# A two-layer recurrent cell: the inverse square root taken as two GpSimd operations of two columns each, and another written-out order of the four streams' operations

## The chip, the cores and the metric

The kernel runs on one core of a Trainium2 chip. The metric is the device time of one execution in microseconds, given as the median of several executions. Work is spread over the core's engines: TensorE (PE, with its weight loads listed apart as PEld), VectorE (DVE), ScalarE (ACT), GpSimd (POOL), and SyncE (SP), whose queue issues most of the transfers. Each engine takes its own instructions strictly in the order in which the kernel lists them.

## What is computed

Four layers work on an array of 256 x 256 positions with 32 channels. The first three (a gated projection and two Sobel-like filters, each behind a group norm) are finished before the part that is changed. The last one is a recurrent network: the first axis counts 256 sequences, the second 256 time steps, and two cells of width H = 128 follow each other in every step. Cut to what matters:

```python
def step(carry, x_t):
    h_all, c_all = carry
    z = x_t @ W_lat + b_lat
    for j in range(2):                                   # two cells (layers)
        zz = concatenate([z, h_all[j]], axis=1) @ W_cell[j] + b_cell[j]
        zz = group_norm(zz)                              # 4 groups of 128: (zz - mu) * rsqrt(var + 1e-5)
        i, f, o, g = split(zz, 4, axis=1)
        c = sigmoid(f) * c_all[j] + sigmoid(i) * tanh(g)
        h = sigmoid(o) * tanh(c)
        z = z + h
    return (new_h, new_c), x_t + z @ W_out + b_out
```

The four groups of the norm are the four gates, so each gate of each sequence has one variance and one scale factor.

## The kernel before

**Streams.** The function `recurrence` (from line 1034) keeps four streams going: layer l (0 or 1) times half h (0 or 1) of the 256 sequences, so that 128 sequences fill the 128 partitions. Below, a name with two digits is an operation of one stream: `h01` is the operation `h` of layer 0, half 1. The means are folded into the weights, so the products in PSUM (`zz`, 128 x 512, four gates side by side) are already deviations from the group's mean.

**One step of a stream** is made by `one` (from line 1112). On PE: for layer 1 `i` (line 1130, the product with the lower layer's state), and `m` (line 1135, with the stream's own last state). Then `sq` (ACT, line 1143, squares of all four gates), `rd` (DVE, line 1148, four sums: tile `ve`, 128 x 4), and `pw` (POOL, line 1151: the power -0.5 of the four sums, tile `rs`, 128 x 4):

```python
rs = v["rs", l, h] = roots[:, 2 * l + h, t % slots, :]
nc.gpsimd.tensor_tensor(rs, get("ve"), inputs.mhalf, ALU.pow)
```

Column g of `rs` is then the scale of the gate activations `si`, `sf`, `so`, `tg` (ACT, line 1124; columns 0 to 3; the output gate's tile is `go`, the others share `ga`). DVE forms `ig` (line 1171), `fc` (line 1175) and the new cell state `c` (line 1179). Two forms end the step. Streams 00 and 10 turn first: PE transposes the output gate (`to`, line 1183) and the cell state (`T`, line 1187), ACT takes the tanh (`th`, line 1190), and DVE multiplies into the turned state hT (`h`, line 1193). Streams 01 and 11 take `th` from c, multiply (`h`, line 1197), transpose (`T`, line 1187), and DVE copies the result out (`e`, line 1199).

**Shared work.** `project` (lines 1100 and 1103; called PROJ below) starts the `zz` of all four streams once per step from the input. `both` (line 1210; `hs`) adds the two layers' states once per step. Once in eight steps `emit` makes the output: `o0` and `o1` (PE, lines 1222 and 1232), `of` (ACT, line 1241), `ot` (DVE, line 1247) and its transfers (line 1251).

**The order.** No scheduler orders this. The table PLAN gives each operation of each stream a due time, OUT those of the shared work; a step's times are shifted by PERIOD = 7.6 per step, all operations of the whole run are sorted by due time and issued in that order, so each engine's queue follows it. The due times are keys of a sort, not times of the chip. Taken modulo 7.6, the steady order in each queue is this (`o0`, `o1`, `of`, `ot` only in one step of eight):

- PE: PROJ m00 T11 i11 m11 to10 T01 i10 T10 m01 to00 (o0) m10 T00 (o1)
- ACT: so11 th11 (of) si01 tg01 sf01 so01 sq00 tg10 th01 so10 si10 sf10 sq11 sf00 so00 th10 si00 tg00 sq01 si11 sf11 tg11 th00 sq10
- DVE: rd10 (ot) h11 ig01 fc01 e11 c01 rd00 h01 ig10 fc10 e01 c10 rd11 fc00 h10 hs ig00 c00 rd01 fc11 ig11 h00 c11
- POOL: pw10 pw00 pw11 pw01

PSUM has eight banks, handed out first in, first out; `zz`, the transposes' target `pt` and the output's `px` each take one.

Of the kernel before, what the change touches and what calls it, by code (L numbers as in the profile page):

```python
# [14 lines left out]
ALU = mybir.AluOpType  # L15
# [4 lines left out]
T = 256  # L20
# [945 lines left out]
class RecurrentInputs:  # L966
# [34 lines left out]
    def of(self, t, rows):  # L1001
# [5 lines left out]


SLOTS = 32
PERIOD = 7.6  # L1010
BLOCKS = 2
PLAN = {
    (0, 0): dict(
        m=0.300, sq=1.315, rd=2.221, pw=2.435, sf=3.687, so=3.851, si=5.257, tg=5.350,
        fc=5.575, to=5.625, ig=5.913, c=6.078, T=7.351, th=7.469, h=7.525,
    ),
    (0, 1): dict(
        m=5.465, sq=5.522, rd=6.135, pw=6.225, si=8.272, tg=8.393, sf=8.539, so=8.617,
        ig=9.064, fc=9.178, c=9.275, th=9.750, h=10.406, T=11.076, e=11.164,
    ),  # L1020
    (1, 0): dict(
        i=11.801, m=14.599, sq=15.182, rd=15.403, pw=15.916, tg=17.278, so=17.665, si=17.826,
        sf=17.853, ig=18.025, to=18.521, fc=18.583, c=18.914, T=19.851, th=20.220, h=20.862,
    ),
    (1, 1): dict(
        i=17.726, m=17.895, sq=18.421, rd=19.343, pw=19.789, si=21.949, sf=21.973, fc=22.060,
        tg=22.379, ig=22.470, c=22.779, so=22.984, th=23.047, h=23.842, T=24.141, e=24.465,
    ),
}
OUT = dict(x=7.840, hs=28.575, o0=29.152, o1=30.235, of=30.667, ot=30.900)  # L1030

def recurrence(tc, out, ident, weights, inputs, general):

    nc = tc.nc
# [33 lines left out]
    def bank(name, key, shape):  # L1070

        k = held[key] = free.pop(0)
        return ps.tile(shape, F32, name=name, tag=f"bank{k}")

    def release(key):
        free.append(held.pop(key))
# [6 lines left out]
    def at(when, what, *args):  # L1083
        todo.append((when, len(todo), what, args))

    first = {k: min(ops[n] for n in ("i", "m") if n in ops) for k, ops in PLAN.items()}
    ahead = {k: floor((when - OUT["x"]) / PERIOD) for k, when in first.items()}
    streams = sorted(first, key=lambda k: first[k] - ahead[k] * PERIOD)

# [21 lines left out]
    def one(name, l, h, t):  # L1111
        seqs = slice(h * P, (h + 1) * P)
        turned = "to" in PLAN[l, h]
        get = lambda k: v[(k, l, h, t) if k == "zz" else (k, l, h)]
        gates = lambda x, g: x[:, g * H : (g + 1) * H]
        four = lambda x: x.rearrange("p (g m) -> p g m", g=4)

        def gate(g, func):

            x, scale = (get("zn"), 1.0) if general else (get("zz"), get("rs")[:, g : g + 1])  # L1120
            if g == 2:
                v["go", l, h] = up.tile([P, H], F32, name="go", bufs=8)
            dst = get("go") if g == 2 else gates(get("ga"), min(g, 2))
            nc.scalar.activation(dst, gates(x, g), func, scale=scale)  # L1124
            v["left", l, h, t] -= 1
            if not v["left", l, h, t]:
                release(("zz", l, h, t))

        if name == "i":
            nc.tensor.matmul(  # L1130
                get("zz"), lhsT=v["hT", 0, t][:, seqs], rhs=wc[:, l, 0, :], start=False, stop=t == 0
            )
        elif name == "m":
            if t:
                nc.tensor.matmul(  # L1135
                    get("zz"),
                    lhsT=v["hT", l, t - 1][:, seqs],
                    rhs=wc[:, l, 1, :],
                    start=False,
                    stop=True,  # L1140
                )
        elif name == "sq":
            nc.scalar.activation(  # L1143
                sqs[l, h, t % 2][:, :, 0:H], four(get("zz")), AF.Square, scale=float(H**-0.5)
            )
        elif name == "rd":
            ve = v["ve", l, h] = sums[:, 2 * l + h, t % slots, :]
            nc.vector.tensor_reduce(ve, sqs[l, h, t % 2], AX.X, ALU.add)  # L1148
        elif name == "pw":
            rs = v["rs", l, h] = roots[:, 2 * l + h, t % slots, :]  # L1150
            nc.gpsimd.tensor_tensor(rs, get("ve"), inputs.mhalf, ALU.pow)  # L1151
            v["ga", l, h] = up.tile([P, 3 * H], F32, name="ga")
            if not general:
                return
            zn = v["zn", l, h] = up.tile([P, 4 * H], F32, name="zn")
            for g in range(4):
                nc.vector.scalar_tensor_tensor(
                    gates(zn, g),
                    gates(get("zz"), g),
                    get("rs")[:, g : g + 1],  # L1160
                    gates(gam[:, l, :], g),
                    ALU.mult,
                    ALU.mult,
                )
            nc.vector.tensor_add(zn, zn, bet[:, l, :])
        elif name in ("si", "sf", "so", "tg"):
            g = ("si", "sf", "so", "tg").index(name)
            gate(g, AF.Tanh if name == "tg" else AF.Sigmoid)
        elif name == "ig":
            c = v["cn", l, h] = sp.tile([P, H], F32, name=f"c{l}{h}")  # L1170
            nc.vector.tensor_mul(c, gates(get("ga"), 0), gates(get("ga"), 2))  # L1171
        elif name == "fc":
            if t:
                fc = v["fc", l, h] = up.tile([P, H], F32, name="fc")
                nc.vector.tensor_mul(fc, gates(get("ga"), 1), get("c"))  # L1175
        elif name == "c":
            c = get("cn")
            if t:
                nc.vector.tensor_add(c, c, get("fc"))  # L1179
            v["c", l, h] = c  # L1180
        elif name == "to":
            v["pt", l, h] = bank("pt", ("pt", l, h), [P, 2, 2 * H])
            nc.tensor.transpose(get("pt")[:, 0, 0:P], get("go"), ident)  # L1183
        elif name == "T":
            if not turned:
                v["pt", l, h] = bank("pt", ("pt", l, h), [P, 2, 2 * H])
            nc.tensor.transpose(get("pt")[:, 1, 0:P], get("c" if turned else "h"), ident)  # L1187
        elif name == "th":
            th = v["th", l, h] = up.tile([P, H], F32, name="th", bufs=8)
            nc.scalar.activation(th, get("pt")[:, 1, 0:P] if turned else get("c"), AF.Tanh)  # L1190
        elif name == "h":
            if turned:
                nc.vector.tensor_mul(hidden(l, t)[:, seqs], get("pt")[:, 0, 0:P], get("th"))  # L1193
                release(("pt", l, h))
            else:
                hh = v["h", l, h] = up.tile([P, H], F32, name="h")
                nc.vector.tensor_mul(hh, get("go"), get("th"))
        elif name == "e":
            nc.vector.tensor_copy(hidden(l, t)[:, seqs], get("pt")[:, 1, 0:P])  # L1199
            release(("pt", l, h))  # L1200

    def hidden(l, t):
        if ("hT", l, t) not in v:
            v["hT", l, t] = hp.tile([P, S], F32, name=f"hT{l}", bufs=5 - l)
        return v["hT", l, t]
# [52 lines left out]
    for k in range(inputs.NX, NB // inputs.XT):  # L1258
        at(((k - inputs.NX + 1) * inputs.XT * J + 4.0) * PERIOD, inputs.load, k)
    at(-1e5, busy, 3)  # L1260
    for n in range(min(ahead.values()), T + max(ahead.values())):
        at(n * PERIOD + OUT["x"], project, n)
    for t in range(T):
        for (l, h), ops in PLAN.items():
            for name, when in ops.items():
                at(t * PERIOD + when, one, name, l, h, t)
        at(t * PERIOD + OUT["hs"], both, t)
    for blk in range(0, NB, BLOCKS):
        for part in ("o0", "o1", "of", "ot"):
            at(((blk + BLOCKS) * J - 1) * PERIOD + OUT[part], emit, blk, part)  # L1270
    todo.sort(key=lambda e: e[:2])
# [45 lines left out]
```

## Time and profile before

| what | value |
|---|---|
| median of 3 runs | 2505.21 us (2502.2 to 2510.31) |
| the profiled execution's own time | 2504.49 us |
| its span in the trace | 2502.6 us |
| mean granted TensorE clock | 0.992 of full speed |
| DVE busy | 2276.8 us (91%) |
| ACT busy | 2247.5 us (90%) |
| POOL busy | 1318.6 us (53%) |
| first `sq` of the recurrent part | at 551.10 us |
| starts of `pw00` from step to step | seven of 7.3 us, then one of 9.05 us, and so on |

In the rows of the timeline the columns are start, duration (both us), engine, line, operation, output <- inputs, shapes, count, and in brackets the idle time before it with what ended it. Neighbours on one engine may overlap: ACT, DVE and PE begin an instruction before the last has fully ended, so the time that an instruction takes from its engine is read from start to start. The groups of instructions give the busy time of a group and the mean ns of one. The chain of waits gives only start, duration, engine and line.

### The profile page before, as it was taken

Reading aid. Unit: us, or ns where it says so; the run is one execution under the profiler, and the core shown is the slowest. Engines: PE = TensorE matmul, PEld = TensorE weight load, DVE = VectorE, ACT = ScalarE, POOL = GpSimd, SP = SyncE. Lnnn points to the kernel's source line nnn. Section 1 sums busy time; section 2 is a strip of 40 time slices with the busy share of each in tenths; the row PEclk is TensorE's granted clock in tenths of the full one; section 3 lists DMA queues with packets and bytes.
Section 4 is the critical chain, followed back from the end, with each engine's and each line's share of the span. In section 5 each row is a group of like instructions: output and inputs, shape, how many; then the busy total and the mean of one; then the engine's idle time right before and its main releaser. Section 6 shows DMA issues by size and latency. Waiting matters only on the chain.

```text
span 2502.6 us, 41399 instructions
## 1 busy us (share of the span) xinstructions
PE 2462.8 (98%) x11615; PEld 1057.6 (42%) x11615; DVE 2276.8 (91%) x6644; ACT 2247.5 (90%) x6876; POOL 1318.6 (53%) x1347
## 2 busy tenths in 40 slices
PE   8999999989999999999999999999999999999997
PEld 4333466653444444444444444444444444444442
DVE  7798898969999999999999999999999999999997
ACT  6788676759999999999999999999999999999996
POOL 1344386845555555555555555555555555555553
PEclk9999999999999999999999999999999999999998
DMA  6877000020010101000010101010101010100000
GB/s 175 49 40 40 2 1 1 1 51 1 5 22 5 23 8 23 10 17 18 9 22 6 22 5 22 5 22 6 22 5 22 5 22 6 22 5 5 5 5 11
DMA packets 117556, 46.71 MB, mean 19 GB/s; under 512 B 77010, under 2 KB 110003, under 8 KB 117316
## 3 DMA queue, kind: packets, MB, share of 16 engines
q1 hardware_dynamic: 115940, 43.80, 12.5%
q8 instruction: 95, 1.56, 0.3%
q14 instruction: 145, 1.19, 0.2%
q10 hardware_dynamic: 1088, 0.13, 0.0%
q0 software_dynamic: 288, 0.03, 0.0%
HBM read 10.37 MB, written 8.39 MB: 7 GB/s over the span
## 4 chain that ended last, share of the span: by engine, by line
PE 77%; DVE 0%; ACT 0%; POOL 0%; issue 0%; DVEq 0%; POOLq 0%; ACTq 0%
PE zz L1135 37%; PE zz L1130 17%; PE zz L1103 9%; PE pt L1187 5%; PE zz L1100 3%; PE pt L1183 2%; PE px L1232 1%; PE px L1222 1%; POOL rs L1151 0%; DVE ve L1148 0%; ACT ga L1124 0%; ACT sq L1143 0%; PE px L1215 0%; DVE c L1171 0%; DVE fc L1175 0%
## 5 line engine op out<-in xcount | busy, mean ns | idle before, releaser
L1151 POOL TENSOR_TENSOR rs<-ve,mhalf 128x4 f32<-128x4 f32 x1024 | 1031.0, 1007 | 920.5 <-DVE ve L1148 920.5
L1135 PE MATMUL zz<-wc,hT 128*128 128x512 f32 x2040 | 1058.6, 606 | 0.7 <-DVE hT L1193 0.7
L1124 ACT ACTIVATE ga<-zz,rs 128x128 f32<-128x128 f32 x3072 | 972.6, 377 | 38.6 <-POOL rs L1151 9.6
L1148 DVE TENSOR_REDUCE ve<-sq 128x4 f32<-128x516 f32 x1024 | 703.5, 687 | 29.1 <-ACT sq L1143 8.0
L1143 ACT ACTIVATE sq<-zz 128x512 f32<-128x512 f32 x1024 | 628.9, 614 | 37.9 <-PE zz L1135 14.4
L1130 PE MATMUL zz<-wc,hT 128*128 128x512 f32 x1024 | 524.1, 594 | 0.0
L1135 PEld LDWEIGHTS zz<-wc,hT 128*128 128x128 f32 x2040 | 328.2, 189 | 398.1 <-DVE c L1179 167.6
L1124 ACT ACTIVATE go<-zz,rs 128x128 f32<-128x128 f32 x1024 | 393.9, 385 | 0.0
L1171 DVE TENSOR_TENSOR c<-ga 128x128 f32<-128x128 f32 x1024 | 299.0, 292 | 61.6 <-ACT ga L1124 31.7
L1179 DVE TENSOR_TENSOR c<-c,fc 128x128 f32<-128x128 f32 x1020 | 287.9, 282 | 9.0
L1175 DVE TENSOR_TENSOR fc<-ga,c 128x128 f32<-128x128 f32 x1020 | 291.9, 286 | 2.9 <-ACT ga L1124 2.9
L1103 PE MATMUL zz<-fx,xt 32*128 32x512 f32 x2048 | 265.6, 588 | 0.0
L472 DVE SCALAR_TENSOR_TENSOR o<-pa,wbias,sg 128x512 f32<-128x512 f32 x256 | 177.4, 744 | 29.7 <-ACT sg L468 19.8
L468 ACT ACTIVATE sg<-pa,wbias 128x512 f32<-128x512 f32 x256 | 160.1, 685 | 44.9 <-PE pa L459 40.2
L1187 PEld LDWEIGHTS pt<-ident,c 128*128 128x128 f32 x512 | 71.1, 139 | 285.1 <-DVE c L1179 276.8
L1190 ACT ACTIVATE th<-c 128x128 f32<-128x128 f32 x512 | 166.2, 325 | 0.4 <-DVE c L1179 0.4
L1190 ACT ACTIVATE th<-pt 128x128 f32<-128x128 f32 x512 | 145.9, 285 | 19.3 <-PE pt L1187 19.3
L1130 PEld LDWEIGHTS zz<-wc,hT 128*128 128x128 f32 x1024 | 161.0, 197 | 2.8 <-issue 0.5
L459 PE MATMUL pa<-xb,wg 32*128 32x512 f32 x512 | 157.7, 649 | 3.5 <-POOL xb L338 3.5
L1193 DVE TENSOR_TENSOR hT<-pt,th 128x128 f32<-128x128 f32 x512 | 145.9, 285 | 15.9 <-ACT th L1190 15.8
L1183 PEld LDWEIGHTS pt<-ident,go 128*128 128x128 f32 x512 | 71.5, 140 | 201.9 <-ACT go L1124 201.9
L1199 DVE COPY hT<-pt 128x128 f32<-128x128 f32 x512 | 145.1, 283 | 8.9 <-PE pt L1187 8.9
(193 smaller groups left out, 2894.4 us busy)
## 6 DMA issues: line engine op xcount, KB each, us to landing
xt<-xa SPq DMA_DIRECT2D x256, 64.0 KB, 2.0
rows<-rstd SPq DMA_DIRECT2D x128, 64.0 KB, 6.4
out_dram<-st SPq DMA_DIRECT2D x252, 32.0 KB, 1.7
nat<-in_x_dram SPq DMA_DIRECT2D x12, 512.0 KB, 10.4
half<-in_x_dram SPq DMA_DIRECT2D x8, 256.0 KB, 7.2
wc<-in_L_conv_W_cell_dram SPq DMA_DIRECT2D x2, 512.0 KB, 5.4
kt<-in_consts_dram SPq DMA_DIRECT2D x1, 640.0 KB, 3.9
kg<-in_consts_dram SPq DMA_DIRECT2D x1, 128.0 KB, 7.8
```

Of the source, the lines that this page charges most:

```text
L1103: nc.tensor.matmul(v["zz", l, h, t], lhsT=inputs.of(t, r), rhs=fx[r, :], start=False, stop=l == 0 and t == 0,)
L1124: nc.scalar.activation(dst, gates(x, g), func, scale=scale)
L1130: nc.tensor.matmul(get("zz"), lhsT=v["hT", 0, t][:, seqs], rhs=wc[:, l, 0, :], start=False, stop=t == 0)
L1135: nc.tensor.matmul(get("zz"), lhsT=v["hT", l, t - 1][:, seqs], rhs=wc[:, l, 1, :], start=False, stop=True,)
L1143: nc.scalar.activation(sqs[l, h, t % 2][:, :, 0:H], four(get("zz")), AF.Square, scale=float(H**-0.5))
L1148: nc.vector.tensor_reduce(ve, sqs[l, h, t % 2], AX.X, ALU.add)
L1151: nc.gpsimd.tensor_tensor(rs, get("ve"), inputs.mhalf, ALU.pow)
L1171: nc.vector.tensor_mul(c, gates(get("ga"), 0), gates(get("ga"), 2))
L1175: nc.vector.tensor_mul(fc, gates(get("ga"), 1), get("c"))
L1179: nc.vector.tensor_add(c, c, get("fc"))
L1187: nc.tensor.transpose(get("pt")[:, 1, 0:P], get("c" if turned else "h"), ident)
L1190: nc.scalar.activation(th, get("pt")[:, 1, 0:P] if turned else get("c"), AF.Tanh)
```

## The change

The power is taken in two operations: `pw` for columns 0 and 1 (gates si and sf), and a new operation `pwb` for columns 2 and 3 (so and tg). The table of due times is replaced throughout. Core of the diff (the branch `general` isn't taken with these inputs):

```diff
-PERIOD = 7.6
+PERIOD = 7.600
 PLAN = {
     (0, 0): dict(
-        m=0.300, sq=1.315, rd=2.221, pw=2.435, sf=3.687, so=3.851, si=5.257, tg=5.350,
-        fc=5.575, to=5.625, ig=5.913, c=6.078, T=7.351, th=7.469, h=7.525,
+        m=0.300, sq=1.475, rd=2.090, pw=2.888, pwb=3.419, si=3.769, sf=3.798, fc=4.338,
+        so=4.419, tg=4.493, ig=4.822, c=4.833, to=5.093, T=5.424, th=6.214, h=6.692,
     ),
     (0, 1): dict(
-        m=5.465, sq=5.522, rd=6.135, pw=6.225, si=8.272, tg=8.393, sf=8.539, so=8.617,
-        ig=9.064, fc=9.178, c=9.275, th=9.750, h=10.406, T=11.076, e=11.164,
+        m=4.605, sq=4.835, rd=5.086, pw=5.520, pwb=6.813, sf=7.880, si=7.991, tg=8.075,
+        so=8.101, fc=8.433, ig=8.752, c=9.517, th=9.888, h=10.336, T=10.648, e=11.260,
     ),
     (1, 0): dict(
-        i=11.801, m=14.599, sq=15.182, rd=15.403, pw=15.916, tg=17.278, so=17.665, si=17.826,
-        sf=17.853, ig=18.025, to=18.521, fc=18.583, c=18.914, T=19.851, th=20.220, h=20.862,
+        i=11.579, m=12.986, sq=13.883, rd=15.300, pw=15.346, sf=17.169, pwb=17.394, so=17.581,
+        si=17.706, tg=17.797, to=18.066, fc=18.100, ig=18.148, c=18.970, T=19.247, th=19.345,
+        h=19.660,
     ),
     (1, 1): dict(
-        i=17.726, m=17.895, sq=18.421, rd=19.343, pw=19.789, si=21.949, sf=21.973, fc=22.060,
-        tg=22.379, ig=22.470, c=22.779, so=22.984, th=23.047, h=23.842, T=24.141, e=24.465,
+        i=16.528, m=17.968, sq=18.616, rd=19.113, pw=19.749, pwb=19.886, si=20.050, sf=20.215,
+        fc=20.675, tg=20.941, ig=21.369, c=22.232, so=22.387, th=23.055, h=23.367, T=23.802,
+        e=24.421,
     ),
 }
-OUT = dict(x=7.840, hs=28.575, o0=29.152, o1=30.235, of=30.667, ot=30.900)
+OUT = dict(x=6.984, hs=31.315, o0=35.060, o1=35.991, of=38.590, ot=42.536)
...
         elif name == "pw":
             rs = v["rs", l, h] = roots[:, 2 * l + h, t % slots, :]
-            nc.gpsimd.tensor_tensor(rs, get("ve"), inputs.mhalf, ALU.pow)
+            now = slice(0, 4 if general else 2)
+            nc.gpsimd.tensor_tensor(
+                rs[:, now], get("ve")[:, now], inputs.mhalf[:, now], ALU.pow
+            )
...
+        elif name == "pwb":
+            if not general:
+                nc.gpsimd.tensor_tensor(
+                    get("rs")[:, 2:4], get("ve")[:, 2:4], inputs.mhalf[:, 2:4], ALU.pow
+                )
```

Sorted in the same way, the new due times give these queues:

- PE: m00 T11 i11 m11 to10 T01 i10 T10 m01 (o0) to00 m10 T00 (o1) PROJ
- ACT: th11 sf01 si01 tg01 so01 (of) sq00 sf10 th01 so10 si10 tg10 sq11 si00 sf00 th10 so00 tg00 sq01 si11 sf11 tg11 th00 sq10 so11
- DVE: rd10 h11 fc01 hs ig01 e11 c01 rd00 h01 fc10 ig10 e01 c10 rd11 fc00 h10 (ot) ig00 c00 rd01 fc11 ig11 h00 c11
- POOL: pw10 pwb10 pw00 pwb00 pw11 pwb11 pw01 pwb01

## The prediction

> **What bounds the kernel now.** I read the page first, for the share of each engine and the costliest groups; then the chain of waits in a stretch of the steady state, for what ends a step; then the timeline of the same stretch, to follow the one loss that I found there back to its source; last the rows of GpSimd alone, for the price of the new operation.
>
> The page, engines and the group of the changed operation:
>
> ```profile
> PE 2462.8 (98%) x11615; PEld 1057.6 (42%) x11615; DVE 2276.8 (91%) x6644; ACT 2247.5 (90%) x6876; POOL 1318.6 (53%) x1347
> ...
> L1151 POOL TENSOR_TENSOR rs<-ve,mhalf 128x4 f32<-128x4 f32 x1024 | 1031.0, 1007 | 920.5 <-DVE ve L1148 920.5
> ```
>
> PE is close to full. The power takes 1007 ns, 1024 times (4 streams x 256 steps), and POOL waits 920 us for its input: it is a link in a chain, not a bound.
>
> The chain of waits, two stretches (start, us, engine, line), one in a normal step, one in the step after an output:
>
> ```profile
> 1527.03 1.06 PE zz L1135 x2
> 1528.09 0.11 PE pt L1187
> 1528.20 0.86 PE zz L1130 x2
> 1529.06 0.86 PE zz L1135 x2
> 1529.92 0.11 PE pt L1183
> 1530.03 0.21 PE pt L1187
> ...
> 1536.19 1.05 PE zz L1135 x2
> ...
> 1539.08 0.11 PE pt L1183
> 1539.19 0.11 PE pt L1187
> ```
>
> The chain is PE throughout. A product takes 0.86, a transpose 0.11. Two rows are longer. m00 (1.06) stands right behind PROJ and loses 0.20; it loses the same (1.05) behind an output, where h00, its input, had ended 1.5 us before (1534.64 against 1536.12), so no order on the other engines cures that. T01 takes 0.21 in a normal step and 0.11 after an output: this 0.10 is a wait. It comes in seven steps of eight, which is why a normal step takes 7.30 and one with output 9.05 = 7.19 + 1.86 (o0 0.86, o1 1.00). So 0.10 x 7 x 32 = 22 us, some 25 with rounding, is all that any order or faster power can gain here while PE's work stays the same.
>
> The timeline, along T01's chain:
>
> ```profile
> 1511.61 1.01 POOL L1151 TENSOR_TENSOR rs<-ve,mhalf 128x4 f32<-128x4 f32 x1 [1.00 <-DVE ve L1148]
> 1512.38 0.31 ACT L1190 ACTIVATE th<-c 128x128 f32<-128x128 f32 x1
> 1512.64 0.88 ACT L1124 ACTIVATE ga<-zz,rs 128x128 f32<-128x128 f32 x3
> 1513.41 0.38 ACT L1124 ACTIVATE go<-zz,rs 128x128 f32<-128x128 f32 x1
> 1513.66 0.61 ACT L1143 ACTIVATE sq<-zz 128x512 f32<-128x512 f32 x1
> 1514.30 0.69 DVE L1148 TENSOR_REDUCE ve<-sq 128x4 f32<-128x516 f32 x1
> 1514.91 0.28 DVE L1197 TENSOR_TENSOR h<-go,th 128x128 f32<-128x128 f32 x1
> 1515.31 0.14 PEld L1187 LDWEIGHTS pt<-ident,h 128*128 128x128 f32 x1
> ```
>
> Read upward: T01's weights (h01) load at 1515.31; h01 stands behind rd00 on DVE (1514.30, and 0.61 from start to start); rd00 waits for sq00 (ends 1514.27); sq00 stands behind the four gates of stream 01 on ACT; the first gate starts at 1512.64, when pw01 ends (1512.62). Without the power it could start at 1512.58, for th11 starts at 1512.38 and a th of this kind holds ACT 0.20 (th01 1514.38, next 1514.58). The power's share in the loss is thus only 0.06; behind it waits ACT itself.
>
> **The price of half a power.** No row shows two columns. The bounds: 0.50 if all of it goes by the column, 1.01 if all is per instruction. Nearest rows, of the same 128x4 shape on POOL:
>
> ```profile
> 30.36 0.19 POOL L225 TENSOR_TENSOR mean_of<-ident,kg 128x4 f32<-128x4 f32 x1
> 30.49 0.30 POOL L226 MEMSET avg<- 128x256 f32 x1
> 30.86 1.03 POOL L228 COPY avg<-mean_of 128x4 f32<-128x4 f32 x8
> ```
>
> The same instruction with a cheap operation takes 0.19, and the next one starts 0.13 later. So 1.01 - 0.19 = 0.82 is the power proper. If it goes by column, a half spans 0.19 + 0.41 = 0.60, and the second starts 0.13 + 0.41 = 0.54 to 0.60 after the first. Against this stands a rule of the Trainium skill (GPSIMD Engine Reference, 3.1 Elementwise, side-by-side cycle accounting): about 2.6 cycles per element for two inputs, beside a fixed dispatch; at its 1.2 GHz an estimated 9 ns for four columns. By it nearly all of 1007 ns would be fixed, halves would cost 1.0 each, and POOL would need 8 x 1.0 = 8.0 us per step of 7.3. The rule is for an add, and the row of 0.19 shows that the fixed part of this shape is small; what it can't show is whether the power's 0.82 has a start-up of its own. I take 0.60, being nearest to the row.
>
> **The change, part by part.** PE's queue is the same round as before (PROJ only counts to the step before; o0 moves one place), so PE's work stays 7.19 per normal step plus the waits. The rest, in the times of the stretch above:
>
> - *Two halves.* Columns 0 and 1 are there at 1511.61 + 0.60 = 1512.21, columns 2 and 3 at about 1512.80. sf01 now starts when ACT is free, 1512.58; si01 follows at 1512.83, tg01 (first reader of the second half) at 1513.08, later than 1512.80; so01 1513.33; sq00 1513.58, above its other floor (m00 ends 1513.48). Then rd00 at 1513.58 + 0.61 + 0.03 = 1514.22, h01 0.61 later, 1514.83 in place of 1514.91. T01's wait falls by 0.07 to 0.08; I take 0.07, leaving 0.03.
> - *hs between fc01 and ig01.* hs holds DVE 0.34 (1509.86 to the next start 1510.20). fc01 (needs sf01, ended 1512.96) stands behind h11 at 1513.08, hs 1513.28, ig01 1513.62, e11 1513.82, c01 1514.02, and DVE is free at 1514.22: just when rd00 can start. I cost it at nothing, but the cover is used up, and each 0.01 more is 0.01 on T01. Bounds: no gain (rd00 can't start sooner), a loss of 0.07 if hs holds DVE for its full 0.41.
> - *Waits that are late next.* With T01 0.07 earlier, T10 needs c10: fc10, ig10, e01, c10 end at about 1516.12, weight load 1516.18, where 1516.26 suffices. to00 needs so00, now behind th10: 1516.72 + 0.36, load 1517.14, where 1517.22 suffices. m11 needs e11, 0.05 later than before, with some 0.12 to spare. Zero each, but none has more than 0.12.
> - *POOL.* 8 x 0.60 = 4.8 us in 7.3; in queue order pwb01 ends 1512.80, before rd10 gives pw10 its input at 1512.95. Nobody waits behind a half.
> - *of behind so01.* It holds ACT 0.57, once in eight steps, in a stretch where o0 and o1 keep PE back: before, sq00 stood idle 0.41 for m00 there although `of` had already been done. Zero; without that cover 0.6 x 32 = 18 us.
> - *ot between h10 and ig00.* This one isn't covered. ot holds DVE 0.64 (1535.87 to 1536.51). Before, it ran right behind an output's o1, with PE still late; now it runs nearly a step later, when the lead is used up. h10 at about 1516.86, ot 1517.07 to 1517.71, ig00 1517.71 (else 1517.37), c00 ends 1518.31, T00's load 1518.37 where 1518.19 suffices: +0.18, once in eight steps. Bounds 0 (if the lead of the output step lasts) and 0.34.
> - *Fill and drain* have the power in the open a few times; under 2 us, taken as zero.
>
> Sum per eight steps: -7 x 0.07 + 0.18 = -0.31; x 32 = -10 us. The profiled execution took 2504.5 (span 2502.6 and 1.9 around it), so 2494.6; the median lies 0.7 higher: 2495. With bounds of these terms (wait wholly gone, ot free: -0.70 x 32 = -22; wait halved, ot 0.34: -0.0): 2482 to 2505.
>
> **Rivals.**
> 1. *The power is mostly per instruction* (slower). Place: tg01, third gate of stream 01, waits for pwb01. With a half of x us it starts at 1511.61 + 2x, and from x = 0.73 on this is later than 1513.08; each 0.05 more costs 0.10 per step, and from about 0.77 the whole gain of T01 is eaten. At 0.85: 0.24 later, so 0.24 + 0.03 - 0.10 = +0.17 per step, x 7 x 32 = +38, with ot +44: 2549. At 1.0 POOL itself needs 8.0 per step: +0.7 x 224 = +157: about 2660. For it: the skill's per-element figure; against it: the 0.19 row. 25% (15% between, 10% at the far end).
> 2. *The wait stays* (no difference). c01's side on DVE (hs) has no slack, to00 and T10 little; if one slips by 0.07, T01's gain is gone and ot's 0.18 remains: 2505 to 2511. 17%.
> 3. *Both halves are waited for.* If a gate waited for the whole row `rs`, sf01 would start at 1512.82, 0.24 late: +0.17 per step, about 2545. Against it: si00 ran (1516.82) while the power of another stream in the same buffer was just being written (1516.90), so waits are kept by region. 4%.
> 4. *All of the wait goes and ot is hidden*: 2483. Speaks for it: T01's remaining 0.03 is within the error of my sum. 14%. The forecast itself: 40%.
>
> **The numbers.** Within 0.3% (7.5 us, 2497.7 to 2512.7) is about what a measurement of this kernel can't tell from no change. Of the forecast's 40% some three quarters lie below 2497.7, with case 4 and a little of 2: faster 0.46. Slower: cases 1 and 3 but for a little that ends near zero, 0.28. Same: 0.26. The range goes from 2482 to 2549, up to case 1's middle, and leaves out its far end; the likeliest case alone is 2485 to 2504.
>
> **What would show it.** Right: the row of 128x2 powers near 600 ns; sf01 0.20 behind th11; T01's row in the chain near 0.13; normal steps near 7.23; one T00 row in eight with about 0.18 more. Wrong: a 128x2 row above 0.75 us, or tg01 ending its wait on POOL; then the time is above 2505. If the halves are short and normal steps still take 7.30, then case 2, and the row that lost its cover is named by the chain.

## The result and the profile after

The changed kernel takes 2499.45 us (median of 15 runs, 2497.3 to 2502.38) against 2505.47 for the kernel before in the same runs: ratio 0.9979, 95% interval 0.9972 to 0.9986. That is 6 us faster, clear of noise but below 0.3%. The prediction was 2495, a gain of 10.

The page of the changed kernel, its span and the two groups that took the place of the old power:

```profile
span 2496.2 us, 42484 instructions
...
L1154 POOL TENSOR_TENSOR rs<-ve,mhalf 128x2 f32<-128x2 f32 x1024 | 705.7, 689 | 538.5 <-DVE ve L1150 519.8
...
L1173 POOL TENSOR_TENSOR rs<-ve,mhalf 128x2 f32<-128x2 f32 x1024 | 742.2, 725 | 0.0
```

A first half takes 0.69, not 0.60 and not 0.50, and a second one 0.73 on average; the second half never waits (idle 0.0 before it). In a row of two halves the second starts 0.65 behind the first (1515.61 and 1516.26 below).

The chain of waits of the changed kernel, one normal step from m00 to T01 (start, us, engine, line; code lines have moved: m is now 1137, i 1132, to 1193, T 1197):

```profile
1530.90 1.06 PE zz L1137 x2
1531.96 0.11 PE pt L1197
1532.07 0.86 PE zz L1132 x2
1532.93 0.86 PE zz L1137 x2
1533.79 0.11 PE pt L1193
1533.90 0.14 PE pt L1197
```

T01, the last row, takes 0.14 where it took 0.21. m00 still takes 1.06, as the prediction said. The step is 7.23 in place of 7.30.

The timeline of the changed kernel along T01's chain, for comparison with the same chain of before:

```profile
1515.61 0.69 POOL L1154 TENSOR_TENSOR rs<-ve,mhalf 128x2 f32<-128x2 f32 x1 [0.60 <-DVE ve L1150]
...
1516.26 0.69 POOL L1173 TENSOR_TENSOR rs<-ve,mhalf 128x2 f32<-128x2 f32 x1
...
1516.38 0.31 ACT L1200 ACTIVATE th<-c 128x128 f32<-128x128 f32 x1
...
1516.59 0.87 ACT L1126 ACTIVATE ga<-zz,rs 128x128 f32<-128x128 f32 x3
...
1517.30 0.41 DVE L1220 TENSOR_TENSOR hs<-hT,hT 128x256 f32<-128x256 f32 x1
1517.34 0.38 ACT L1126 ACTIVATE go<-zz,rs 128x128 f32<-128x128 f32 x1
...
1517.59 0.61 ACT L1145 ACTIVATE sq<-zz 128x512 f32<-128x512 f32 x1
```

The first gate (ga, 1516.59) starts 0.21 behind th11 (1516.38); before it was 0.26 (1512.38 to 1512.64). The first half had ended at 1516.30, so the gate now waits for ACT alone. The second half ends at 1516.95, and its first reader tg01, third of the three gates, starts at about 1517.09: 0.14 to spare.

The loss is in one step of eight. From one power of stream 01 (pw01) to the same one a step later the trace gives 7.23 us as a rule, but across an output 9.37 and then 7.26; before the change it was 7.30, and across an output 9.06 and then 7.30. (The 9.05 in the table of before is this stream's; the starts of pw00 are 9.01 and then 7.35 apart there.) The chain leaves PE in the step after the output:

```profile
1544.43 0.01 DVE hT L1203
1544.45 0.05 issue
1544.50 0.05 DVEq L1257
1544.55 0.05 issue
1544.59 0.05 DVEq L1257
1544.64 0.05 issue
1544.69 0.05 DVEq L1257
1544.74 0.04 issue
1544.79 0.71 DVE st L1257
1545.50 0.18 DVE c L1181
1545.68 0.02 issue
1545.71 0.30 DVE c L1189
1546.01 0.04 issue
1546.05 0.33 PE pt L1197
```

DVE starts h10 (hT) at 1544.41; its queue then spends a third of a microsecond on waits in front of ot (DVEq, line 1257), so that ot starts 0.38 behind h10, where an operation of this size lets the next one start after 0.20 to 0.21 in this stretch; then comes ot itself (0.71), then ig00 and c00, and only then can PE transpose c00 (0.33 in place of 0.11). This is the uncovered place that the prediction named, at about twice its price. Before the change the same waits cost nothing: in that trace they stand at 1534.85 to 1535.20, while DVE was at work on rd10 (1534.84 to 1535.53), and ot had to wait for `of` until 1535.87 anyway.

The sums over eight steps (32 powers) are the handiest figure, since most of them repeat to 0.02: 60.16 to 60.17 before, 60.03 after. So about 0.14 x 32 = 4.5 us of the 6.4 by which the two spans differ lie in the recurrence's blocks. The first power operation starts 2.1 earlier (550.5 in place of 552.7), which is about the rest; that lies ahead of everything that was changed, and the traces of the ten kernels here have it anywhere from 547.5 to 554.2. The 6 us of the medians is thus more than the recurrence itself shows; both figures lie in the interval (3.5 to 7 us).

### The profile page after: what moved, and what is told of

Its sections match the earlier page's. It is cut to its first block, busy times and chain, and to the rows that moved or that the text cites. A ratio compares the mean times of both kernels' runs of the same rounds, so it can differ in the third digit from the quotient of the medians.

```text
span 2496.2 us, 42484 instructions
## 1 busy us (share of the span) xinstructions
PE 2452.5 (98%) x11615; PEld 1036.2 (42%) x11615; DVE 2242.0 (90%) x6644; ACT 2243.5 (90%) x6876; POOL 1697.2 (68%) x2371
## 4 chain that ended last, share of the span: by engine, by line
PE 71%; DVE 4%; ACT 2%; issue 1%; POOL 0%; DVEq 0%; ACTq 0%; POOLq 0%
PE zz L1137 34%; PE zz L1132 15%; PE zz L1105 9%; PE pt L1197 5%; PE zz L1102 3%; PE pt L1193 2%; PE px L1242 1%; ACT ga L1126 1%; PE px L1232 1%; DVE ve L1150 1%; DVE st L1257 1%; DVE c L1189 1%; DVE c L1181 1%; ACT go L1126 0%; ACT th L1200 0%
## 5 line engine op out<-in xcount | busy, mean ns | idle before, releaser
L1154 POOL TENSOR_TENSOR rs<-ve,mhalf 128x2 f32<-128x2 f32 x1024 | 705.7, 689 | 538.5 <-DVE ve L1150 519.8
L1126 ACT ACTIVATE ga<-zz,rs 128x128 f32<-128x128 f32 x3072 | 961.9, 370 | 7.7 <-POOL rs L1154 7.4
L1173 POOL TENSOR_TENSOR rs<-ve,mhalf 128x2 f32<-128x2 f32 x1024 | 742.2, 725 | 0.0
L1145 ACT ACTIVATE sq<-zz 128x512 f32<-128x512 f32 x1024 | 620.7, 606 | 39.8 <-PE zz L1137 16.7
L1137 PEld LDWEIGHTS zz<-wc,hT 128*128 128x128 f32 x2040 | 317.4, 190 | 337.2 <-DVE c L1189 176.5
L1126 ACT ACTIVATE go<-zz,rs 128x128 f32<-128x128 f32 x1024 | 384.9, 376 | 0.3 <-POOL rs L1173 0.3
L1132 PEld LDWEIGHTS zz<-wc,hT 128*128 128x128 f32 x1024 | 160.7, 197 | 11.3 <-issue 9.5
```

The lines of the kernel that those rows point to most:

```text
L1132: nc.tensor.matmul(get("zz"), lhsT=v["hT", 0, t][:, seqs], rhs=wc[:, l, 0, :], start=False, stop=t == 0)
L1137: nc.tensor.matmul(get("zz"), lhsT=v["hT", l, t - 1][:, seqs], rhs=wc[:, l, 1, :], start=False, stop=True,)
L1145: nc.scalar.activation(sqs[l, h, t % 2][:, :, 0:H], four(get("zz")), AF.Square, scale=float(H**-0.5))
L1154: nc.gpsimd.tensor_tensor(rs[:, now], get("ve")[:, now], inputs.mhalf[:, now], ALU.pow)
L1173: nc.gpsimd.tensor_tensor(get("rs")[:, 2:4], get("ve")[:, 2:4], inputs.mhalf[:, 2:4], ALU.pow)
```

## The experiments

Theory: the split power takes the power out of T01's chain, worth 0.07 per step, provided the gates that go first read the half that comes first; and ot's new place gives most of it back. Rivals: the order alone, or the split alone, gives the gain; the long step has another cause than ot. The kernels of the first four experiments ran beside one another (kernel before: 2507.8 there), and so did the last four (2506.47).

**1. of and ot put back.**

```diff
-OUT = dict(x=6.984, hs=31.315, o0=35.060, o1=35.991, of=38.590, ot=42.536)
+OUT = dict(x=6.984, hs=31.315, o0=35.060, o1=35.991, of=38.265, ot=38.500)
```

> The changed kernel with the output's two steps put back where they stood before: of right behind th11, ot right behind rd10. My theory: ot between h10 and ig00 costs 0.35 us once in eight steps (9.37 + 7.26 from power to power, where a stall-free pair would be 9.05 + 7.23), 32 times 11 us. So 2488 us, 0.7% under the kernel before, and no T00 row of 0.33 in the chain. Rival, that the long pair comes from the halves of the power on a loaded POOL: no difference to the changed kernel, 2499.

Measured: 2492.58, ratio 0.9942 (0.993 to 0.9954). Eight steps take 59.69 in place of 60.03: 0.34 x 32 = 11 us, as expected from the trace; the median came out 4.6 higher than my 2488. About half of that is the level of these runs, in which the kernel before took 2507.8 and not 2505.47; in the trace the recurrence also starts 3.7 later than in that of the changed kernel (first power at 554.2).

**2. ot alone moved.**

```diff
-OUT = dict(x=6.984, hs=31.315, o0=35.060, o1=35.991, of=38.590, ot=42.536)
+OUT = dict(x=6.984, hs=31.315, o0=35.060, o1=35.991, of=38.590, ot=39.400)
```

> The changed kernel with ot alone moved, between ig01 and e11 behind its of, into the 0.91 us in which DVE waits there for T11 in the step after an output. If ot's place is the cost and that of of is free: 2488 to 2491 (e11 may be 0.1 late). If of's new place costs too: 2493 or more.

Measured: 2490.99, ratio 0.9938 (0.9926 to 0.995); eight steps 59.69, the same as in experiment 1. In the step after the output, m10 and T00 now follow each other without a wait:

```profile
1540.39 0.86 PE zz L1137 x2
1541.25 0.11 PE pt L1197
```

T00 (second row) is back at 0.11. The place of ot is the whole cost, that of `of` is free.

**3. The new order with the power whole.** `pw` takes all four columns again, `pwb` does nothing.

```diff
-            now = slice(0, 4 if general else 2)
+            now = slice(0, 4)
...
         elif name == "pwb":
-            if not general:
-                nc.gpsimd.tensor_tensor(
-                    get("rs")[:, 2:4], get("ve")[:, 2:4], inputs.mhalf[:, 2:4], ALU.pow
-                )
+            pass
```

> The changed order, but the power whole again (four columns in one operation, pwb empty). Theory (order and halves both needed, the halves give little): the first gate sf01 starts behind the power, at 0.65 + 0.36 after its input, 0.04 later than with halves, so T01's wait grows from 0.03 to 0.07: +0.04 x 7 x 32 = +9, about 2508. Rival, that the order alone gave the gain: 2499. Rival, that the halves gave all of it: 2515.

Measured: 2515.54, ratio 1.0034 (1.0022 to 1.0047), slower than the kernel before. My number was a miss and the second rival's right. The chain of waits of this kernel:

```profile
1538.42 0.86 PE zz L1137 x2
1539.28 0.11 PE pt L1190
1539.39 0.21 PE pt L1194
```

T01 is back at 0.21, as before the change, and the step at 7.31. Eight steps take 60.54. The long step of stream 01 is 9.37 here too, so ot's price is in it; without ot's 0.34 this would be 60.20, close to the 60.17 of before (worked out: no kernel had the whole power with ot moved). The new order alone gives nothing; within it, the halves are worth all of the 0.07 per step. I had counted 0.04, from the delay of the first gate against th11 in one place; it measured 0.27 (1521.72 to 1521.99) against 0.21, so 0.06, and T01's row grew by 0.07.

**4. The halves with the order of before.** PLAN and OUT are those of before, with `pwb` directly behind `pw` in every stream (each due time of `pw` plus 0.001), for example:

```diff
-        m=0.300, sq=1.315, rd=2.221, pw=2.435, sf=3.687, so=3.851, si=5.257, tg=5.350,
+        m=0.300, sq=1.315, rd=2.221, pw=2.435, pwb=2.436, sf=3.687, so=3.851, si=5.257, tg=5.350,
```

> The order of before, the power in two halves back to back. Theory: tg01 and tg10, second gates of their streams there, read the second half, which comes 1.34 us after the power's start in place of 1.01. tg10 is held 0.25 and th01 stands behind it on ACT, h01 about 0.12 to 0.2 late, every step: 2530 to 2550, slower than before. Rival, that halves are worth 0.06 on their own because the first gate comes earlier: 2490 to 2495.

Measured: 2585.03, ratio 1.0311 (1.0295 to 1.0327). The direction is right, the size was too small: 77 us slower than the kernel before in the same runs, where I had expected 22 to 42. The timeline shows three places where ACT waits for the second half, or a reader waits for ACT because of it:

```profile
1520.50 0.29 DVE L1179 TENSOR_TENSOR c<-ga 128x128 f32<-128x128 f32 x1 [0.23 <-ACT ga L1124]
...
1521.64 0.37 ACT L1124 ACTIVATE ga<-zz,rs 128x128 f32<-128x128 f32 x1 [0.16 <-POOL rs L1171]
...
1522.28 0.80 POOL L1152 TENSOR_TENSOR rs<-ve,mhalf 128x2 f32<-128x2 f32 x1 [0.67 <-DVE ve L1148]
...
1523.04 0.81 POOL L1171 TENSOR_TENSOR rs<-ve,mhalf 128x2 f32<-128x2 f32 x1
...
1523.88 0.37 ACT L1124 ACTIVATE go<-zz,rs 128x128 f32<-128x128 f32 x1 [0.16 <-POOL rs L1171]
```

The three waiting rows are ig01 (behind tg01), tg10 and so00. I had counted only the second. The halves were longer than I had counted, too: 1.57 for the pair of stream 00 (1522.28 to 1523.85, the two POOL rows) and 1.45 for that of stream 10, not 1.34. The delays add up, for the step becomes a loop that hardly touches PE: the chain of waits of this stretch gives DVE's sums 25.8% and the two halves of the power 11.4% and 10.4%. A normal step takes 7.65 (pw10 starts at 1527.82 and 1535.47).

**5. Three columns and one,** on the kernel of experiment 2: `pw` takes columns 0 to 2, `pwb` column 3.

```diff
-            now = slice(0, 4 if general else 2)
+            now = slice(0, 4 if general else 3)
...
-                    get("rs")[:, 2:4], get("ve")[:, 2:4], inputs.mhalf[:, 2:4], ALU.pow
+                    get("rs")[:, 3:4], get("ve")[:, 3:4], inputs.mhalf[:, 3:4], ALU.pow
```

> The kernel with ot alone moved, but the power cut three columns and one instead of two and two. Price of the operation: from 1.007 us for four columns and 0.689 for two, 0.16 per column on 0.37 fixed: so 0.85 for three and 0.53 for one. My theory, that the first operation only has to be done before th11 lets go of ACT (0.98 us after the power's start) and the second before tg01 (1.48 after it): 0.85 and about 1.34 still fit, so the step stays 7.23 and the time within 2 us of the kernel with two and two (2491). Rival, that every 0.01 of the first operation counts: 0.16 later in the step, so 7.3 and more, over 2510.

Measured: 2493.07, ratio 0.9948 (0.9935 to 0.9962), beside 2490.99 for two and two in the other group of runs; eight steps 59.71 to 59.74 against 59.69. The groups of instructions:

```profile
L1154 POOL TENSOR_TENSOR rs<-ve,mhalf 128x3 f32<-128x3 f32 x1024 | 877.5, 857 | 532.3 <-DVE ve L1150 521.3
L1173 POOL TENSOR_TENSOR rs<-ve,mhalf 128x1 f32<-128x1 f32 x1024 | 563.3, 550 | 0.0
```

The chain of waits, to10 and T01:

```profile
1531.59 0.11 PE pt L1193
1531.69 0.14 PE pt L1197
```

One, two, three and four columns take 0.55, 0.69, 0.86 and 1.01: about 0.16 per column on a fixed 0.37. And 0.17 more in the first operation costs next to nothing, 0.03 in eight steps, and T01 stays at 0.14: the first operation has to be done before ACT is free, and no sooner.

**6. ot in the changed place, its waits taken earlier.** One DVE memset of one column of st stands between ig01 and e11, in the gap that DVE has there in that step.

```diff
-OUT = dict(x=6.984, hs=31.315, o0=35.060, o1=35.991, of=38.590, ot=42.536)
+OUT = dict(x=6.984, hs=31.315, o0=35.060, o1=35.991, of=38.590, os=39.400, ot=42.536)
...
+        elif part == "os":
+            st = v["st"] = op.tile([P, BLOCKS * S], F32, name="st")
+            nc.vector.memset(st[:, 0:1], 0.0)
         else:
-            st = op.tile([P, BLOCKS * S], F32, name="st")
+            st = v["st"]
```

> The changed kernel with ot where the change has it, plus one DVE memset of one column of st between ig01 and e11 (0.1 us, where DVE is idle in that step), so that the waits for the earlier transfers from st are taken there and not in front of ot. Theory: ot's long price (0.35 in place of my 0.18) holds four queue instructions of some 0.1 us in front of ot; without them the long pair of steps falls from 16.63 by about 0.15, x 32 = 5 us: 2494 to 2495. Rival, that ot's own 0.64 on DVE makes the whole price: 2499.

Measured: 2493.0, ratio 0.9952 (0.9939 to 0.9966). The timeline:

```profile
1542.24 0.29 DVE L1203 TENSOR_TENSOR hT<-pt,th 128x128 f32<-128x128 f32 x1
...
1542.45 0.70 DVE L1260 STREAM_TRANSPOSE st<-fin 128x512 f32<-128x512 f32 x1
...
1543.07 0.25 DVE L1181 TENSOR_TENSOR c<-ga 128x128 f32<-128x128 f32 x1
```

ot starts 0.21 behind h10, where it was 0.38 (1544.41 to 1544.79). The semaphore waits stand in front of the memset in this trace and none is left in front of ot. Eight steps take 59.84: 0.19 less than with the change, 0.15 more than with ot out of the way. So of ot's 0.34, the queue's waits were 0.19 and ot itself 0.15.

**7. hs put back as well,** on the kernel of experiment 1.

```diff
-OUT = dict(x=6.984, hs=31.315, o0=35.060, o1=35.991, of=38.265, ot=38.500)
+OUT = dict(x=6.984, hs=34.900, o0=35.060, o1=35.991, of=38.265, ot=38.500)
```

> The kernel with of and ot put back, and hs too put back to where it stood before, between h10 and ig00: what remains of the new order is that of the gates and the swaps of fc and ig. Theory: hs between fc01 and ig01 is just covered by sq00, so nothing changes: step 7.23, time within 2 us of the kernel with of and ot put back (2492.6). Rival, that hs uses up part of T01's gain: the step falls towards 7.20, time to 2486. Other rival, that hs in its new place was needed: 7.26 or more.

Measured: 2490.13, ratio 0.9937 (0.9923 to 0.995); eight steps 59.67 to 59.70, steps 7.23. hs in its new place costs nothing and brings nothing. What is left of the new order here is that of the gates, th10 ahead of so00, o0 ahead of to00, and fc and ig swapped in streams 01 and 10. Which of these the halves need, beyond the gates of experiment 4, was not tried one by one.

**8. An attempt at T01's last 0.03,** on the kernel of experiment 2: on ACT sq00 ahead of so01, th01 ahead of sf10.

```diff
-        so=8.101, fc=8.433, ig=8.752, c=9.517, th=9.888, h=10.336, T=10.648, e=11.260,
+        so=9.090, fc=8.433, ig=8.752, c=9.517, th=9.888, h=10.336, T=10.648, e=11.260,
...
-        i=11.579, m=12.986, sq=13.883, rd=15.300, pw=15.346, sf=17.169, pwb=17.394, so=17.581,
+        i=11.579, m=12.986, sq=13.883, rd=15.300, pw=15.346, sf=17.500, pwb=17.394, so=17.581,
```

> The kernel with ot alone moved, and on ACT sq00 ahead of so01, th01 ahead of sf10. An attempt at the 0.03 that T01 still loses: sq00 may start when m00 is done, 0.05 earlier, so rd00 and h01 are earlier and T01's row falls to 0.11. Against it: sf10 and with it so10, si10 and tg10 come about 0.2 later, ig10 and c10 too, and T10 had some 0.1 to spare: then T10's row grows by 0.1. I expect the second to win: step 7.26 to 7.32, time 2498 to 2515; if T10 has more to spare than that, 7.20 and 2484.

Measured: 2551.47, ratio 1.0182 (1.0168 to 1.0196), slower; the step is 7.47, beyond my range. The chain of waits:

```profile
1538.95 0.23 PE pt L1193
1539.18 0.11 PE pt L1197
1539.29 0.86 PE zz L1132 x2
1540.15 0.27 PE pt L1197
```

T01 (second row) is at 0.11, as meant, but T10 (last) waits 0.16, as feared, and to10 (first) 0.12, which I had not counted: its input so10 stands behind the moved sf10. Here 0.03 won for one stream was paid for with 0.28 in another.

## Why the prediction was right, and where it was off

- *What bounds the step, and how much can be had:* right. Steps after the change are 7.23 as worked out, m00's 0.20 stayed in every kernel tried whose chain runs through it (what causes it was not tested), and no kernel tried got below 7.23 as a lasting step.
- *T01's wait falls by 0.07:* right in size (0.21 to 0.14, as forecast to the last digit) and in cause. Whole power in the new order brings 0.21 back (experiment 3), and a first operation of 0.86 leaves it at 0.14 (experiment 5): the first gate waits for ACT, not for POOL.
- *Half a power costs 0.60:* too low, it is 0.69, with a fixed 0.37 of which the row of the cheap operation showed 0.19. The power has a start-up of its own, which I had said that row couldn't rule out. It did no harm only because it stayed 0.04 under the 0.73 at which I had put the turn; that margin was luck, since the estimate was off by 0.09. The rival at 1.0, by the Trainium skill's figure for an add (GPSIMD Engine Reference, 3.1 Elementwise, side-by-side cycle accounting), fell: the power takes 0.16 us per column, where that figure gives an estimated 2 ns, so it does not carry over from the add to the power.
- *hs costs nothing:* right (experiment 7). *`of` costs nothing:* right (experiment 2).
- *ot costs 0.18:* the place was right, the size not. This is the term behind the difference between 10 us and 6: the prediction had -0.49 + 0.18 = -0.31 per eight steps, and the trace has -0.14; ot's 0.34 in place of 0.18 makes 0.16 of the 0.17 between them. The 0.18 counted ot's own time, which measured 0.15; the waits that its queue makes for the earlier transfers from st, 0.19 (experiment 6), were put at nothing. They had cost nothing in the old place, so ot's row in the trace of before did not show them.
- *The T01 term over eight steps:* right. With ot out of the way, eight steps lose 60.17 - 59.69 = 0.48 against the 0.49 forecast.
- *Rivals:* none came true. That a gate might wait for the whole row `rs` is excluded by the first gate starting at 1516.59 while the second half ran until 1516.95.
- *The chances:* the prediction drew the line to "no difference" at 2497.7 and gave "faster" 0.46 and "same" 0.26; by that line 2499.45 is "same". The line was drawn too wide: with 15 runs on each side, 6 us was clear of noise.

The gain of the halves in their new order, with ot out of the way, is 0.48 x 32 = some 15 us, 0.6%; the change gave a good two thirds of that back (0.34 of 0.48) by moving one operation that happens once in eight steps.

## What to carry to other kernels

Here splitting a slow operation paid only up to the point where its consumer's engine was free, and only because the order of the consumers was changed with it: neither the halves nor the new order brought anything alone, and the halves alone cost 3%. In an order written out by hand, cost the rare operations as carefully as those of every step, with the waits in front of them, and put them where their own engine has to wait anyway, as DVE does for T11 in the step after an output (experiment 2).

## What was not expected of the hardware

The waits of one DVE instruction for several transfers took 0.34 us of its queue here (1544.45 to 1544.79), 0.19 of which showed in the time, although those transfers had ended long before: they read what the output eight steps earlier had written, and the last whose end is recorded had landed at 1490.5.

In the changed kernel a power of two columns took 0.69 in every first half but 0.76 to 0.77 in the second half of streams 10 and 11 (1503.22, 1507.02). It is not the stream that decides: with hs moved back (experiment 7) stream 10's second half took 0.69 (1506.66) and only that of stream 11 still 0.77 (1503.24), and with the order of before (experiment 4) both halves of stream 00 took some 0.8. So it depends on what the other engines do beside it, and moving one DVE operation was enough to change it. Which neighbour lengthens it, and how, stays open.
